# Moving the closing work of an attention unit to other steps of the next one

## The chip, the core and the metric

The kernel runs on one core of a Trainium2 chip. Its time is device time in microseconds (us), from the first to the last work of the program. The kernel before was run three times, 3617.6 to 3618.77 us, with a median of 3618.65 us. A profiled execution, which the profile describes, is one run more. The engines are TensorE (PE in the profile; PEld is its weight load), VectorE (DVE), ScalarE (ACT), GpSimd (POOL) and SyncE (SP, which here only starts DMAs).

## What is computed

Two graph layers over x of 8 batches, 2048 nodes and 256 features, all in float32. The first is a graph convolution with batch norm; the second is masked attention with 4 heads of 64. Each ends in a residual and a layer norm. Cut to what matters here:

```python
def _L1_gnn_ref(h, W, adj):
    qkv = h @ W                                   # 256 -> 3 x 256
    q, k, v = ...                                 # 4 heads of 64
    mask = jnp.where(adj == 0, -jnp.inf, 0.0)
    scores = einsum('bhid,bhjd->bhij', q, k) / np.sqrt(64) + mask
    attn = softmax(scores, axis=-1)
    return einsum('bhij,bhjd->bhid', attn, v)

x = _layernorm(x + _L0_gnn_ref(x, adj, ...))      # convolution, batch norm, twice
x = _layernorm(x + _L1_gnn_ref(x, L1_gnn_W, adj))
```

## The kernel before, in words

The convolution's part fills the first 1270 us or so and is not touched. The attention's part is cut into 64 units: 8 batches, in each of them 2 pairs of heads (`hp`), and for each pair 4 chunks (`c`) of 512 query rows. So a batch has eight units, which this text numbers 0 to 7: units 0 to 3 are the first pair's chunks, 4 to 7 the second pair's.

A unit has 16 steps, one for each tile of 128 keys. In a step TensorE makes the scores of the step three ahead (L842, into one of two `st` tiles in PSUM) and weighs the values with the exponentials of the present step (L872, into the single `out_ps` tile). Both use the array as four tiles of 64x64. VectorE adds the mask (L854), ScalarE takes the exponential (L860), in one of 13 `prob` tiles. The softmax uses no maximum; the sums of the exponentials are made on the side: an accumulating DMA started by GpSimd adds neighbouring steps' tiles in pairs (L882), GpSimd adds the pairs (L884, L891, L893) into `acc`, and TensorE adds over the partitions.

All four computing engines keep the order in which the program writes their work. A step is written as: scores, at step 15 the weighing and the result's copies (L897, L898), the masking, the exponentials, then the side tasks of that step, then the weighing, then the adding up. Side tasks are put in a table by `at_step(u, j, f, ...)`: task `f` belongs to step `int(j)` of unit `u`, and tasks of one step are ordered by `j`. A side task on TensorE therefore stands between the scores and the weighing of its step, and everything behind it on TensorE waits with it. The side tasks:

- Closing a unit, in the next one: `finish_sums` (L909, four products into the 32-column quarters, then ScalarE's copy into `sm`, L917), `finish_turn_sums` (two transposes L923, VectorE's copy L925 and reciprocal L930), `finish_turn` (four transposes L936 of the result) and `finish` (VectorE adds the scaled result to x1, L944, in halves).
- Closing a chunk of rows, after its second pair of heads: `emit_stats` (L660, L662 on VectorE, in halves), `root` (four small instructions on GpSimd, L97, L99, L667, L668) and `emit` (two applies L672 on ScalarE for each half, after the second one the output's DMA).
- Bringing in the next batch, a chunk at a time in units 3 to 7: `load_y` and `load_x` (DMAs on SP), `bn` (L696 on ScalarE, two), `norm` (four transposes L711 for each half, then VectorE's add L719 and the statistics), `root`, `apply` (L672) and `turn` (four transposes L740 for each half, then ScalarE's copy into `x1t`, L746).
- `project` (L777 for Q and K, L791 for V), at 0.1, 6.1 and 10.1 of a unit by the list `PROJECT`.

Every side product of TensorE goes into a PSUM tile named `pm`, of which there are two in turn: a third one has to wait until the first has been read. There are seven x1 tiles (`NCH + 3`), one `yt` tile and two `sm` tiles. In the last unit four of the 16 exponentials' tiles are summed by TensorE directly.

Of the kernel before, what the change touches and what calls it, by code (L numbers as in the profile page):

```python
# [8 lines left out]
F32 = mybir.dt.float32  # L9
# [17 lines left out]
def tile_gcn_then_masked_attention(  # L27
# [18 lines left out]
    P = 128  # L46
    B, N, D = x.shape
# [3 lines left out]
    NT = N // P  # L51
# [4 lines left out]
    NCH = N // CH  # L56
    TPC = CH // P
# [139 lines left out]
    with tc.tile_pool(name="bt7", bufs=1, side="right") as bp7, tc.tile_pool(  # L197
        name="stage", bufs=2, side="right"
    ) as sp, tc.tile_pool(name="stage1", bufs=1, side="right") as sp1, tc.tile_pool(
        name="pst", bufs=4, space=PSUM  # L200
# [80 lines left out]
    with tc.tile_pool(  # L281
        name="psa", bufs=4, space=PSUM
    ) as psa, tc.tile_pool(name="psh", bufs=3, space=PSUM) as psh, tc.tile_pool(
        name="psd", bufs=1, space=PSUM
# [94 lines left out]
        for v, (k, b, d) in enumerate(units):  # L379
            first, last = v == 0, v == len(units) - 1  # L380
            turn = not last and units[v + 1][0] != k
            w = v + 1
# [257 lines left out]
    BR = 256  # L640
# [168 lines left out]
    def attention():  # L809


        with tc.tile_pool(
            name="attn_in", bufs=2, side="left", reuse_waits="tile"
        ) as ip, ExitStack() as late, tc.tile_pool(
            name="ps_s", bufs=2, space=PSUM, reuse_waits="tile"
        ) as ps_s, tc.tile_pool(
            name="ps_o", bufs=1, space=PSUM, reuse_waits="tile"
        ) as ps_o, tc.tile_pool(
            name="ps_m", bufs=2, space=PSUM, reuse_waits="tile"
        ) as ps_m:  # L820
            inp = Layer1Input(ip, ps_m, NCH + 3)
            units = [(b, hp, c) for b in range(B) for hp in range(HP) for c in range(NCH)]
            probs, accs, outs, ots, sts, pms = {}, {}, {}, {}, {}, {}

# [5 lines left out]
            def on_pe(u):  # L830
                return 4 if u == NU - 1 else 0
# [68 lines left out]
            def finish_sums(u):  # L900

                pm = ps_m.tile([P, BR], F32, name="pm")
                parts = [probs.pop(g) for g in range((u + 1) * NT - on_pe(u), (u + 1) * NT)]
                parts.append(accs.pop(u))
                for n, part in enumerate(parts):
                    for h in range(2):
                        for q in range(2):
                            r0 = 32 * (2 * h + q)
                            nc.tensor.matmul(  # L909
                                pm[r0 : r0 + 32, :], ones[:, :32],  # L910
                                part[:, h, q * BR : (q + 1) * BR],
                                start=(n == 0), stop=(n == len(parts) - 1),
                            )
                for g in range(u * NT, (u + 1) * NT - on_pe(u)):
                    del probs[g]
                sts[u] = ap_.tile([P, BR], F32, name="sm")
                nc.scalar.copy(sts[u], pm)  # L917

            def finish_turn_sums(u):
# [50 lines left out]
            def at_step(u, j, f, *args):  # L970
                tasks = side.setdefault((u, int(j)), [])
                tasks.append((j, f, args))
                tasks.sort(key=lambda task: task[0])

            per_b = HP * NCH
            for u in range(NU):
                b, hp, c = units[u]
                at_step(u + 1, 4.1, finish_sums, u)
                at_step(u + 1, 6, finish_turn_sums, u)
                at_step(u + 1, 6.2, finish_turn, u)  # L980
                at_step(u + 1, 6.2, finish, u, 0)
                at_step(u + 1, 7, finish, u, 1)
                if u == NU - 2:
                    for half in range(2):
                        at_step(u + 1, 8.3 + half, inp.emit_stats, b, c, half)
                        at_step(u + 1, 13 + half, inp.emit, b, c, half)
                    at_step(u + 1, 10.5, inp.root, b, c)
                elif u == NU - 1:
                    for half in range(2):
                        at_step(u + 1, 6.3 + half, inp.emit_stats, b, c, half)  # L990
                        at_step(u + 1, 6.4 + half, inp.root_half, b, c, half)
                        at_step(u + 1, 8 + half, inp.emit_half, b, c, half)
                    at_step(u + 1, 10, count_sums)
                elif hp == HP - 1:
                    for half in range(2):
                        at_step(u + 1, 10.3 + 3 * half, inp.emit_stats, b, c, half)
                        at_step(u + 2, 3 + half, inp.emit, b, c, half)
                    at_step(u + 2, 2, inp.root, b, c)

            PROJECT = (0.1, 6.1, 10.1)

            def project_at(u, b, hp, c):
                for w in range(3):

                    later = 0
                    if w == hp == 0:
                        later = 10.1 if c == NCH - 1 else NT
                    at_step(u + (later == NT), PROJECT[w] + later % NT, inp.project, b, hp, c, w)  # L1010

            for b in range(B):
                u0 = b * per_b
                if b:
                    project_at(u0, b, 0, NCH - 1)
                for c in range(NCH):
                    project_at(u0 + 1 + c, b, 1, c)
                    if b + 1 == B:
                        continue
                    u = u0 + 3 + c  # L1020
                    at_step(u, 1, inp.load_y, b + 1, c)
                    at_step(u, 5, inp.load_x, b + 1, c)
                    for o in range(NO):
                        at_step(u, 5 + o, inp.bn, b + 1, c, o)
                    at_step(u, 10, inp.norm, b + 1, c, 0)
                    at_step(u + 1, 0, inp.norm, b + 1, c, 1)
                    at_step(u + 1, 4, inp.root, b + 1, c)
                    for half in range(2):
                        at_step(u + 1, 7 + half, inp.apply, b + 1, c, half)
                    at_step(u + 1, 10.2, inp.turn, b + 1, c, 0)  # L1030
                    at_step(u + 2, 4, inp.turn, b + 1, c, 1)
                    if c < NCH - 1:
                        project_at(u + 2, b + 1, 0, c)

# [13 lines left out]
            with tc.manual_schedule(engines=IN_ORDER):  # L1048
                for c in range(NCH):
                    inp.yt[0, c] = y0[c]  # L1050
                    inp.x1[0, c] = ip.tile([P, TPC, D], F32, name="x1", bufs=NCH + 3)
                    for o in range(NO):
                        inp.bn(0, c, o)

                def ready(c):
                    pm = ps_s.tile([P, TPC, D], F32, name="st")
                    for half in range(2):
                        pmh = pm[:, half * IT : (half + 1) * IT, :]
                        inp.turn_y(0, c, half, pmh)
                        inp.add_y(0, c, half, pmh, x0[c])  # L1060
                    inp.root(0, c)

                def halves(f, c):
                    for half in range(2):
                        f(0, c, half)

                for c in range(NCH - 1):
                    ready(c)
                halves(inp.apply, 0)
                halves(inp.turn, 0)  # L1070
                halves(inp.apply, 1)
                inp.project(0, 0, 0, 1, k_on_act=True)
                inp.project(0, 0, 0, 0)
                ready(NCH - 1)
                right.close()
                ap_ = inp.y_pool = late.enter_context(
                    tc.tile_pool(name="attn", bufs=2, side="right", reuse_waits="tile")
                )
                inp.project(0, 0, 0, 2)
                halves(inp.turn, 1)  # L1080
                for g in range(LEAD):
                    mask_scores(g, scores(g))
                    exps(g)
                    if g == 1:
                        inp.project(0, 0, 1, 1)
                        halves(inp.apply, 2)
                for g in range(NU * NT):
                    u, j = divmod(g, NT)
                    ahead = g + LEAD < NU * NT
                    if ahead:  # L1090
                        st = scores(g + LEAD)
                    if j == NT - 1:
                        weigh(g)
                        finish_out(u)
                    if ahead:
                        mask_scores(g + LEAD, st)
                        exps(g + LEAD)
                    for _, f, args in side.get((u, j), ()):
                        f(*args)
                    if j < NT - 1:  # L1100
                        weigh(g)
                    add_up(g)
                for u in (NU, NU + 1):
                    for j in range(NT):
                        for _, f, args in side.get((u, j), ()):
                            f(*args)
# [125 lines left out]
```

## Time and profile before

| | us |
|---|---|
| median of three runs | 3618.65 |
| the profiled execution | 3617.16 |
| its span, on which the profile's shares are taken | 3615.4 |
| TensorE matmuls busy | 3553.4 |
| GpSimd busy | 2267.2 |
| VectorE busy | 1985.4 |
| ScalarE busy | 1638.9 |
| a unit of the attention, depending on its side work | 35.1 to 38.1 |
| a unit of the last batch's second half, without projections | 29.7 to 32.0 |

The page of a profile gives each engine's busy time, the chain of work that ended last and the costliest groups of instructions. The list of waits says which group waited for which, with the sum, the number and the longest. The timeline lists instructions in order of time: start, duration, engine, line, operation, what it writes and reads, and in brackets the idle time before it and what ended it. The ends of matmuls are modelled and overlap the next ones, so times on TensorE are best read from start to start.

### The profile page before, as it was taken

To read this page: it belongs to the slowest core of one execution; us is meant where nothing else is said; L and a number is where in the kernel's file an instruction comes from. 1 tells how busy PE (TensorE), PEld (TensorE's weight loads), DVE (VectorE), ACT (ScalarE), POOL (GpSimd) and SP (SyncE) were. 2 spreads that over 40 slices of the span, in tenths; PEclk is the share of its full clock that TensorE was granted. 3 is DMA by queue.
4 is the path that set the end of the run, shared out by engine and by line. 5 is a ranking of instruction groups with operands and counts; after the bars stand their busy time and mean duration, and the time that the engine had idled before them with its cause. 6 is when DMAs were issued, how large, how long until landed. Compare 5 with 4: busy or idle time off the path is not lost.

```text
span 3615.4 us, 55155 instructions
## 1 busy us (share of the span) xinstructions
PE 3553.4 (98%) x22503; PEld 1468.3 (41%) x22503; DVE 1985.4 (55%) x2929; ACT 1638.9 (45%) x2036; POOL 2267.2 (63%) x1530
## 2 busy tenths in 40 slices
PE   8999999999999899999999999999999999999997
PEld 5444444444444443433333433343333333343332
DVE  6212141221146656766766776676676676676666
ACT  5101100110134455655665665565565565566555
POOL 3543263424247647776767686777777777777777
PEclk9999999999999999999999999999999999999999
DMA  9222232231246345656565566565656566555555
GB/s 337 70 70 87 81 134 82 76 99 29 82 190 263 143 91 107 125 123 123 114 143 112 117 134 129 112 139 119 117 123 133 113 127 131 117 118 123 111 109 115
DMA packets 197142, 440.14 MB, mean 122 GB/s; under 512 B 14080, under 2 KB 121104, under 8 KB 186384
## 3 DMA queue, kind: packets, MB, share of 16 engines
q0 software_dynamic: 64656, 239.37, 34.9%
q1 hardware_dynamic: 132048, 196.11, 15.8%
q8 instruction: 178, 2.92, 0.3%
q10 hardware_dynamic: 176, 1.06, 0.1%
q14 instruction: 84, 0.69, 0.1%
HBM read 126.62 MB, written 75.51 MB: 56 GB/s over the span
## 4 chain that ended last, share of the span: by engine, by line
PE 92%; ACT 3%; POOL 2%; DVE 2%; issue 1%; DMA 0%; POOLq 0%; ACTq 0%; SPq 0%; DVEq 0%
PE out_ps L872 23%; PE st L842 22%; PE pa L333 21%; PE pm L777 6%; PE ph L366 5%; PE pa L543 5%; PE pm L791 3%; PE pm L909 1%; PE pm L740 1%; ACT x L672 1%; DVE prob L854 1%; POOL acc L893 1%; ACT prob L860 1%; PE pm L711 1%; PE pm L936 1%; PE pm L923 1%
## 5 line engine op out<-in xcount | busy, mean ns | idle before, releaser
L854 DVE SCALAR_TENSOR_TENSOR prob<-mask,st 128x1024 f32<-128x1024 uint8 x1024 | 1241.1, 1218 | 588.0 <-PE st L842 585.0
L860 ACT ACTIVATE prob<-prob 128x1024 f32<-128x1024 f32 x1024 | 1079.5, 1056 | 910.9 <-DVE prob L854 795.5
L872 PE MATMUL out_ps<-prob,v 64*64 64x512 f32 x8192 | 1075.7, 595 | 1.7 <-DVE ot L898 1.7
L842 PE MATMUL st<-qt,kt 64*64 64x512 f32 x8192 | 1063.5, 589 | 1.7 <-DVE prob L854 1.3
L893 POOL TENSOR_TENSOR acc<-acc,prob 128x1024 f32<-128x1024 f32 x319 | 831.5, 2607 | 5.1
L333 PE MATMUL pa<-t,x 128*128 128x512 f32 x1792 | 772.1, 593 | 2.7 <-ACT x L309 2.7
L882 POOL DMA_DIRECT2D prob<-prob x447 | 403.1, 908 | 590.0 <-PE out_ps L872 518.8
L842 PEld LDWEIGHTS st<-qt,kt 64*64 64x64 f32 x8192 | 311.1, 133 | 572.9 <-issue 515.8
L333 PEld LDWEIGHTS pa<-t,x 128*128 128x128 f32 x1792 | 341.0, 190 | 431.8 <-issue 427.7
L872 PEld LDWEIGHTS out_ps<-prob,v 64*64 64x64 f32 x8192 | 287.5, 132 | 523.2 <-issue 453.8
L414 POOL TENSOR_TENSOR ag<-ag,dbc 128x512 f32<-128x512 f32 x16 | 20.2, 1262 | 484.9 <-DVE ag L413 452.2
L884 POOL TENSOR_TENSOR acc<-acc,prob 128x1024 f32<-128x1024 f32 x126 | 297.8, 2363 | 9.9
L370 ACT ACTIVATE h<-ph,b1s 128x512 f32<-128x512 f32 x112 | 76.9, 687 | 404.4 <-PE ph L366 404.4
L777 PE MATMUL pm<-x1t,wq 128*128 128x512 f32 x512 | 244.7, 601 | 0.7 <-ACT x1t L746 0.7
L394 ACT COPY ag<-pa 128x512 f32<-128x512 f32 x16 | 9.4, 585 | 421.5 <-PE pa L333 408.1
L366 PE MATMUL ph<-ag,w1s 128*128 128x512 f32 x448 | 193.4, 592 | 0.0
L891 POOL TENSOR_TENSOR acc<-prob 128x1024 f32<-128x1024 f32 x64 | 172.3, 2692 | 0.0
L672 ACT ACTIVATE x<-x,ln_nm,ln_rs 128x256 f32<-128x256 f32 x256 | 137.9, 587 | 31.9 <-POOL ln_nm L668 31.9
L371 DVE BATCH_NORM_STATS2 st<-h 128x6 f32<-128x512 f32 x112 | 76.9, 692 | 99.1 <-ACT h L370 99.1
L791 PEld LDWEIGHTS pm<-wq,x1t 128*128 128x128 f32 x1024 | 119.2, 192 | 28.5 <-issue 26.8
L366 PEld LDWEIGHTS ph<-ag,w1s 128*128 128x128 f32 x448 | 85.1, 190 | 107.1 <-issue 106.9
L791 PE MATMUL pm<-wq,x1t 128*128 128x128 f32 x1024 | 128.4, 278 | 0.0
(139 smaller groups left out, 2571.8 us busy)
## 6 DMA issues: line engine op xcount, KB each, us to landing
prob<-prob POOLq DMA_DIRECT2D x447, 512.0 KB, 4.7
x<-in_x_dram SPq DMA_DIRECT2D x92, 512.0 KB, 5.2
h_d<-h SPq DMA_DIRECT2D x28, 1024.0 KB, 3.9
t<-h_d SPq DMA_DIRECT2D x28, 1024.0 KB, 8.1
a<-in_adj_dram SPq DMA_DIRECT2D x16, 1024.0 KB, 5.0
y_d<-ag SPq DMA_DIRECT2D x32, 512.0 KB, 2.6
out_dram<-x SPq DMA_DIRECT2D x31, 512.0 KB, 5.9
yt<-y_d SPq DMA_DIRECT2D x28, 512.0 KB, 3.3
```

The costliest lines, as they stand in the source:

```text
L333: nc.tensor.matmul(pa, s.t[:, m, :], t[:, m, :], start=(m == 0), stop=(m == HT - 1))
L366: nc.tensor.matmul(ph, w1s[:, d, f * P : (f + 1) * P], ag[:, d, :], start=(d == 0), stop=(d == ND - 1),)
L543: nc.tensor.matmul(py, w[:, f, :], t[:, f, :], start=(f == 0), stop=(f == 1))
L777: nc.tensor.matmul(pm, wq[:, d, wcols], xt[:, d, cols], start=(d == 0), stop=(d == ND - 1))
L791: nc.tensor.matmul(pm[:, j * P : (j + 1) * P], xt[:, d, t * P : (t + 1) * P], wq[:, d, wcols], start=(d == 0), stop=(d == ND - 1),)
L842: nc.tensor.matmul(st[r * HD : (r + 1) * HD, h, :], kt[hs, j * P + r * HD : j * P + (r + 1) * HD], qt[hs, cols], start=True, stop=True,)
L854: nc.vector.scalar_tensor_tensor(p, mask[:, j, cols][:, None, :].to_broadcast([P, 2, CH]), MASKED, st, op0=ALU.mult, op1=ALU.add,)
L860: nc.scalar.activation(probs[g], probs[g], AF.Exp)
L872: nc.tensor.matmul(outs[u][hs, r, :], inp.qkv[b, hp][2][rs, j, hs], probs[g][rs, h, :], start=(j == 0), stop=(j == NT - 1),)
L882: nc.gpsimd.dma_start(probs[g - 1], probs[g], accum_op=ALU.add)
L884: nc.gpsimd.tensor_add(accs[u], accs[u], probs[g])
L893: nc.gpsimd.tensor_add(accs[v], accs[v], probs[g - 5])
```

## The change

It moves side tasks to other steps and changes two buffer counts. No instruction is added or taken away in the attention's work. In the next unit, the sums go from step 4 to step 6, their transposes and the result's from step 6 to step 10, around the V projection, and the additions to x1 from steps 6 and 7 to 10 and 11. A finished chunk's statistics go to steps 12 and 14, its root to step 15 of that same unit (before: step 2 of the next), its applies from steps 3 and 4 to 4 and 5. For the next batch's chunks, x is loaded at step 1 and not 5, `bn` goes to steps 3 and 4, the first half of `norm` from step 10 to 6, the root from 4 to 3, and both halves of `turn` to step 13 (before: step 10 and step 4 of the next unit). The Q projection of the first pair of heads is no longer put off. There are eight x1 tiles and one `sm` tile.

```diff
-            inp = Layer1Input(ip, ps_m, NCH + 3)
+            inp = Layer1Input(ip, ps_m, NCH + 4)
...
-                sts[u] = ap_.tile([P, BR], F32, name="sm")
+                sts[u] = ap_.tile([P, BR], F32, name="sm", bufs=1)
...
-                at_step(u + 1, 4.1, finish_sums, u)
-                at_step(u + 1, 6, finish_turn_sums, u)
-                at_step(u + 1, 6.2, finish_turn, u)
-                at_step(u + 1, 6.2, finish, u, 0)
-                at_step(u + 1, 7, finish, u, 1)
+                at_step(u + 1, 6, finish_sums, u)
+                at_step(u + 1, 10, finish_turn_sums, u)
+                at_step(u + 1, 10.2, finish_turn, u)
+                at_step(u + 1, 10.3, finish, u, 0)
+                at_step(u + 1, 11, finish, u, 1)
                 if u == NU - 2:
                     for half in range(2):
-                        at_step(u + 1, 8.3 + half, inp.emit_stats, b, c, half)
-                        at_step(u + 1, 13 + half, inp.emit, b, c, half)
-                    at_step(u + 1, 10.5, inp.root, b, c)
+                        at_step(u + 1, 11.3 + half, inp.emit_stats, b, c, half)
+                        at_step(u + 1, 14 + half, inp.emit, b, c, half)
+                    at_step(u + 1, 12.5, inp.root, b, c)
                 elif u == NU - 1:
                     for half in range(2):
-                        at_step(u + 1, 6.3 + half, inp.emit_stats, b, c, half)
-                        at_step(u + 1, 6.4 + half, inp.root_half, b, c, half)
-                        at_step(u + 1, 8 + half, inp.emit_half, b, c, half)
-                    at_step(u + 1, 10, count_sums)
+                        at_step(u + 1, 10.4 + half, inp.emit_stats, b, c, half)
+                        at_step(u + 1, 10.5 + half, inp.root_half, b, c, half)
+                        at_step(u + 1, 12 + half, inp.emit_half, b, c, half)
+                    at_step(u + 1, 14, count_sums)
                 elif hp == HP - 1:
                     for half in range(2):
-                        at_step(u + 1, 10.3 + 3 * half, inp.emit_stats, b, c, half)
-                        at_step(u + 2, 3 + half, inp.emit, b, c, half)
-                    at_step(u + 2, 2, inp.root, b, c)
+                        at_step(u + 1, 12.5 + 1.5 * half, inp.emit_stats, b, c, half)
+                        at_step(u + 2, 4 + half, inp.emit, b, c, half)
+                    at_step(u + 1, 15.5, inp.root, b, c)
...
             def project_at(u, b, hp, c):
                 for w in range(3):
-                    later = 0
-                    if w == hp == 0:
-                        later = 10.1 if c == NCH - 1 else NT
-                    at_step(u + (later == NT), PROJECT[w] + later % NT, inp.project, b, hp, c, w)
+                    at_step(u, PROJECT[w], inp.project, b, hp, c, w)
...
                     at_step(u, 1, inp.load_y, b + 1, c)
-                    at_step(u, 5, inp.load_x, b + 1, c)
+                    at_step(u, 1, inp.load_x, b + 1, c)
                     for o in range(NO):
-                        at_step(u, 5 + o, inp.bn, b + 1, c, o)
-                    at_step(u, 10, inp.norm, b + 1, c, 0)
+                        at_step(u, 3.5 + 1.2 * o, inp.bn, b + 1, c, o)
+                    at_step(u, 6.2, inp.norm, b + 1, c, 0)
                     at_step(u + 1, 0, inp.norm, b + 1, c, 1)
-                    at_step(u + 1, 4, inp.root, b + 1, c)
+                    at_step(u + 1, 3, inp.root, b + 1, c)
                     for half in range(2):
                         at_step(u + 1, 7 + half, inp.apply, b + 1, c, half)
-                    at_step(u + 1, 10.2, inp.turn, b + 1, c, 0)
-                    at_step(u + 2, 4, inp.turn, b + 1, c, 1)
+                        at_step(u + 1, 13 + 0.2 * half, inp.turn, b + 1, c, half)
```

More of the change, by code (lines that the diff above doesn't have):

```diff
@@ L1050, in attention @@
                     inp.yt[0, c] = y0[c]
-                    inp.x1[0, c] = ip.tile([P, TPC, D], F32, name="x1", bufs=NCH + 3)
+                    inp.x1[0, c] = ip.tile([P, TPC, D], F32, name="x1", bufs=NCH + 4)
                     for o in range(NO):
```

## The prediction

> **What bounds the kernel now.** I read the page's busy times and chain first, then the list of waits, then the timeline of single units of the attention, which start at 1272.8 us and fill the last 2343 us.
>
> ```profile
> PE 3553.4 (98%) x22503; PEld 1468.3 (41%) x22503; DVE 1985.4 (55%) x2929; ACT 1638.9 (45%) x2036; POOL 2267.2 (63%) x1530
> ...
> PE 92%; ACT 3%; POOL 2%; DVE 2%; issue 1%; DMA 0%; POOLq 0%; ACTq 0%; SPq 0%; DVEq 0%
> ```
>
> TensorE is the bound: only 62 us of the span are without a matmul, so a gain has to come from TensorE's few gaps and from what it loses between kinds of product. The waits name a gap that the change aims at, and one behind it:
>
> ```profile
> ACT x L672 <- POOL ln_nm L668: 31.9, 33, 4.8
> ...
> PE pm L923 <- ACT sm L917: 17.1, 31, 1.6
> ```
>
> The transposes of the sums (L923) wait for ScalarE's copy of the sums (L917). The timeline of one unit with input work gives the prices (start, duration; PE rows overlap, so I read start to start):
>
> ```profile
> 2020.31 1.04 PE L842 MATMUL st<-qt,kt 64*64 64x512 f32 x8
> ...
> 2021.16 1.04 PE L872 MATMUL out_ps<-prob,v 64*64 64x512 f32 x8
> ...
> 2022.02 1.04 PE L842 MATMUL st<-qt,kt 64*64 64x512 f32 x8
> ...
> 2022.99 0.64 PE L909 MATMUL pm<-acc,ones 128*32 128x256 f32 x8
> ...
> 2023.20 1.22 DVE L854 SCALAR_TENSOR_TENSOR prob<-mask,st 128x1024 f32<-128x1024 uint8 x1 [0.56 <-PE st L842]
> ...
> 2023.56 1.09 PE L872 MATMUL out_ps<-prob,v 64*64 64x512 f32 x8
> ...
> 2024.45 1.06 ACT L860 ACTIVATE prob<-prob 128x1024 f32<-128x1024 f32 x1 [0.68 <-DVE prob L854]
> 2024.47 1.04 PE L842 MATMUL st<-qt,kt 64*64 64x512 f32 x8
> ...
> 2025.42 0.35 ACT L917 COPY sm<-pm 128x256 f32<-128x256 f32 x1
> ...
> 2027.15 0.44 PE L923 MATMUL pm<-ident,sm 128*128 128x128 f32 x2
> ...
> 2027.43 1.88 PE L777 MATMUL pm<-x1t,wq 128*128 128x512 f32 x4
> ...
> 2029.15 0.60 PE L936 MATMUL pm<-ident,ot 128*128 128x128 f32 x4
> ...
> 2029.68 1.09 PE L872 MATMUL out_ps<-prob,v 64*64 64x512 f32 x8
> ```
>
> A plain step is 1.717 us (20.31 to 22.02). Any side product in it makes the scores 0.97 instead of 0.86 and the weighing 0.91 instead of 0.86: 0.16 us for leaving and re-entering the 64x64 shape. The sums take 0.57. From scores' start to the end of the sums' copy is 3.75 us (22.02 to 25.77), because ScalarE must first run that step's exponentials.
>
> [...] A projection alone takes 1.91, last in a group 1.81, in its middle 1.72; four transposes 0.44, plus 0.06 if first and 0.09 if last. [...]
>
> **The change, part by part**, in the execution profiled (3617.16 us; span 3615.4; the median of the runs, 3618.65, is 1.5 above it). I number the eight units of a batch 0 to 7; inputs of the next batch enter in units 3 to 7. Before, the first scores of batch 4's units start at 2450.77, 2488.82, 2524.66, 2559.76, 2595.25, 2631.57, 2667.50, 2704.67, and the next batch at 2741.44: 38.05, 35.84, 35.10, 35.49, 36.32, 35.93, 37.17, 36.77, together 290.67. Sixteen plain steps are 27.48; the rest is side work.
>
> Groups of side work. Before: steps 0, 4, 6, 10 in all eight units (32 per batch). After: 0, 6, 10 in all, 13 in units 4 to 7 (28). From these prices:
> - Step 0: Q projection 0.16 + 1.91 = 2.07 in units 0 to 3; with the transposes of norm's second half, 0.16 + 0.49 + 1.81 = 2.47 in units 4 to 7. Unit 5 gets the Q projection that now doesn't wait a unit (its own step 0 was bare and lost 0.84 to the result's copies, which a projection covers); unit 0 loses its second one.
> - Step 6: sums 0.57, then K projection. No row shows a projection right after the 128x32 sums: its entry costs 0 to 0.10. In the adjacency stage 16 transposes after such products take 1.90 (17.01 to 18.90) for 16 x 0.109 = 1.75, so entry and exit are paid there; I take 0.10. Units 0, 1, 2, 7: 0.16 + 0.57 + 1.91 = 2.64.
> - Step 10: sums' transposes 0.27, V projection 1.79, result's transposes 0.53, in and out 0.16: 2.75. The V projection lies between the sums' transposes and the result's, so the wait for VectorE's copy of the former is covered (it ends at 2.6 us of the step, needed at 3.0). Without it: 1.3 per unit, from 1.24 to 2.6.
> - Step 13: eight transposes, 0.16 + 1.02 = 1.18, units 4 to 7. ScalarE's two copies of them (0.58 each) end at 4.7 us, before step 14's exponentials can start at 5.3; if ScalarE were late there, the result's copy at step 15 would be late by as much.
>
> What goes: the wait at L923. The sums are copied at step 6 and needed at step 10, over 6 us later. In batch 4 that wait was 0.65, 0.74, 0.25 and 0.25 in units 0, 1, 6, 7.
>
> What is late next: in units 3 to 6 norm's first half is now at step 6, behind sums and K projection. It takes the third `pm` of that step, and there are two, so its transposes wait until the sums' tile is copied. They could start at 0.97 + 0.57 + 1.82 = 3.36 us; the copy ends at 3.75, they start at 3.80. Behind them stands the step's weighing, so TensorE stops. Step 6 adds 3.80 + 0.53 + 0.91 - 1.72 = 3.52 in units 3 to 5, where ScalarE is not behind (the two batch-norm activations, 0.80 each, are at steps 3 and 4, and a plain step leaves it about 0.7 us). In unit 6 the finished chunk's two applies (1.08 each) also fall at steps 4 and 5. From the exponentials of step 3, which start 2.72 before step 6: 0.97, 0.78, 0.97, 0.98, 0.78, 0.97, 0.98, 0.97, then the copy 0.35 ends at 5.04. Step 6 adds 5.09 + 0.53 + 0.91 - 1.72 = 4.81. Of this, 0.44 three times and 1.73 once are stall: 3.1 us per batch, as much as the old waits cost.
>
> After, then: units 0 to 2 are 27.48 + 2.07 + 2.64 + 2.75 = 34.94; unit 3 35.82; units 4 and 5 37.39; unit 6 38.68; unit 7 36.52. Sum 290.62 against 290.67: nothing. Batches 1 to 6 took 1747.2 before (three of them had a longer wait somewhere), 6 x 290.62 = 1743.7: -3.4. Batch 0, units 1 to 7: 256.0 before; after, with the Q projections at step 3 of units 1 and 2 that stay, 259.8: +3.8, since no finished chunk made it wait in units 0 and 1. Batch 7 has no inputs: units 0 to 4 179.2 before, 174.7 after: -4.5. Units 5 to 7 were 30.81, 32.00, 29.66; the sums' wait for the accumulator (0.57, as they stood at step 4) and the transposes' wait (1.18 in the last two) go: -0.5, -1.7, -1.75.
>
> The tail: the second-last chunk's root is moved from step 10 to 12 of the last unit, behind GpSimd's add of step 11 and ahead of its last two adds. It needs statistics which VectorE, with two maskings in between, ends at about 28 us of the unit; root 1.95, two adds 2.4 each: accumulator done at 35.0, before at 34.5 (3600.1). So unit 7 and tail end +0.5 and not -1.75.
>
> Costed at nothing: the root at step 15 puts 1.95 us ahead of GpSimd's last adds, done then 13.1 us after that step's start, and the sums ask at 14.1 or later; at the old step 4 it would have stalled them. It takes ScalarE's wait at L672 away. Loads of y and x both go out at step 1 on SP; the y lands in 3.1 to 5.6 us and is needed 9 us later. An eighth x1 buffer frees the x load from the output's DMA. One `sm` buffer: read four steps before it is rewritten. Statistics at steps 12 and 14 leave VectorE 1 us late at most, which the two `st` tiles just hold.
>
> Sum: -3.4 + 3.8 - 4.5 - 0.5 - 1.7 + 0.5 = -5.8, to 3611.4 for that execution and 3612.9 beside the median. With entry at 0, 3.2 lower.
>
> **Rivals.** (A) ScalarE is quicker than worked out, or norm's tile is free: no stall at step 6. Against it: exponentials precede the copy in ScalarE's order. It would save 21 x 0.44 + 7 x 1.73 = 21.4 more: 3591.5. (B) Slower: the same stall is deep in all four units as in unit 6, because a batch-norm activation waits for its y, now needed two steps earlier and loading beside x, and holds ScalarE's queue. That is 21 x 1.3 = 27 more: 3640. For it: 1 us of lateness there is 1 us of TensorE. It decides from a mean stall of 1.2 us (0.76 worked out), or a y landing over 9 us. Against: longest landing 5.6. (C) Fewer groups and waits do not show, as rows on TensorE were only redistributed: 3618.7.
>
> **Numbers.** Main case 0.66, A 0.10, B 0.20, C 0.04. A measurement tells about 0.2% (7.2 us) from nothing. The main case's own range is 3606 to 3620, with 0.38 of it beyond -7.2: faster 0.25 + 0.10 = 0.35, same 0.40 + 0.04 = 0.44, slower 0.21. The range for 8 in 10 is 3599 to 3632: it leaves out most of A and the upper half of B.
>
> **What would show it.** L923 waiting for L917 gone; the transposes of norm (L711) waiting for L917 28 times, about 21 us in all, longest 1.7; unit sums of 290.6; 28 fewer groups. It is wrong if L711 doesn't wait, if ScalarE waits for y, or if the accumulator is late at step 6.

## The result: the forecast effect, less than one measurement could tell from nothing

The changed kernel took 3614.6 us (median of four runs, 3613.77 to 3615.44), the kernel before 3618.56 (median of four). The ratio is 0.999, with a 95% interval of 0.9972 to 1.0007. The profiled execution took 3614.43 us, with a span of 3612.6. Its page (busy time, then the chain by engine, then the group of the applies):

```profile
PE 3553.4 (98%) x22503; PEld 1469.7 (41%) x22503; DVE 1994.5 (55%) x2929; ACT 1635.0 (45%) x2036; POOL 2265.8 (63%) x1530
...
PE 95%; ACT 2%; DVE 2%; POOL 1%; DMA 0%; issue 0%; DVEq 0%; POOLq 0%; ACTq 0%; SPq 0%
...
L672 ACT ACTIVATE x<-x,ln_nm,ln_rs 128x256 f32<-128x256 f32 x256 | 137.6, 586 | 10.5 <-POOL ln_nm L668 10.5
```

TensorE's busy time is that of before to the last digit, so the busy row tells nothing here. ScalarE's wait for the root, 31.9 us before, is 10.5. The list of waits (waiter <- releaser: us in all, times, longest) has the two that matter:

```profile
PEld pm L711 <- ACT sm L917: 38.9, 28, 2.2
...
PE pm L711 <- ACT sm L917: 15.7, 28, 1.4
...
PEld pm L923 <- ACT sm L917: 1.2, 1, 1.2
```

The transposes of the sums (L923) wait for the sums' copy once, in the tail, instead of 31 times. The transposes of `norm` (L711) wait for that same copy 28 times: the four units with inputs of seven batches. The weight load's 38.9 us count from its own last load, when products are still being made, and the matmul row's 15.7 depends on modelled ends (unit 6 of batch 4 has 2.23 and 1.40 in these rows, and 1.57 from start to start). What the wait costs is read from start to start below: 20 us.

First scores to first scores, the units 0 to 7 of each of the batches 1 to 6 take 34.94, 34.94, 34.94, 35.87, 37.45, 37.45, 38.57 and 36.52 us (within 0.01 in every batch), together 290.68; before, batch 4 had 290.67. So an undisturbed batch gains nothing, as forecast. Nearly all of what batches 1 to 6 gain comes from batches 2, 3 and 6, which took 291.70, 291.94 and 291.37 us before (291.77, 291.98 and 291.45 in experiment 1). The old wait was deeper there: in unit 0 of batch 2 and unit 7 of batch 3 GpSimd's additions, and with them its root, ended 1.1 and 1.3 us later than in the same units of batch 4, so that ScalarE's applies and the copy of the sums came later too, and L923 waited 1.59 and 1.46 us instead of 0.57 and 0.19. Why GpSimd was late in these batches stays open. The whole span, before against after:

| stretch | before | after | difference | forecast |
|---|---|---|---|---|
| up to the first scores of the attention | 1272.77 | 1275.34 | +2.57 | 0 |
| batch 0 | 303.68 | 307.56 | +3.88 | +3.8 |
| batches 1 to 6 | 1747.14 | 1744.05 | -3.09 | -3.4 |
| batch 7, units 0 to 4 | 179.19 | 174.69 | -4.50 | -4.5 |
| batch 7, units 5 and 6 | 62.81 | 60.47 | -2.34 | -2.2 |
| last unit and tail | 49.8 | 50.5 | +0.7 | +0.5 |

The head, which the change doesn't touch, took back two fifths of what the attention gained. In the timelines of before and then of after it is this line (start, duration), the projections of Q and K for the first unit, and the first scores behind it:

```profile
1264.14 3.70 PE L777 MATMUL pm<-x1t,wq 128*128 128x512 f32 x8 [0.67 <-ACT x1t L746]
...
1272.77 1.95 PE L842 MATMUL st<-qt,kt 64*64 64x512 f32 x16
```

```profile
1264.39 6.02 PE L777 MATMUL pm<-x1t,wq 128*128 128x512 f32 x8 [0.67 <-ACT x1t L746]
...
1275.34 1.95 PE L842 MATMUL st<-qt,kt 64*64 64x512 f32 x16
```

The same eight products take 2.3 us more; the mean granted clock from 1262 to 1280 us was 0.94 before and 0.80 after.

The step the forecast turned on is step 6. The timeline of after, batch 4: first unit 5 (the step begins at 2645.84), then unit 6 (it begins at 2683.28), in rows of TensorE and ScalarE:

```profile
2645.84 1.04 PE L842 MATMUL st<-qt,kt 64*64 64x512 f32 x8
...
2646.80 0.64 PE L909 MATMUL pm<-acc,ones 128*32 128x256 f32 x8
...
2648.27 1.06 ACT L860 ACTIVATE prob<-prob 128x1024 f32<-128x1024 f32 x1 [0.68 <-DVE prob L854]
2649.23 0.35 ACT L917 COPY sm<-pm 128x256 f32<-128x256 f32 x1
...
2649.64 0.66 PE L711 MATMUL pm<-ident,yt 128*128 128x128 f32 x4 [0.28 <-ACT sm L917]
2650.22 1.09 PE L872 MATMUL out_ps<-prob,v 64*64 64x512 f32 x8
...
2682.28 1.06 ACT L860 ACTIVATE prob<-prob 128x1024 f32<-128x1024 f32 x1
...
2683.24 1.08 ACT L672 ACTIVATE x<-x,ln_nm,ln_rs 128x256 f32<-128x256 f32 x2
2683.28 1.04 PE L842 MATMUL st<-qt,kt 64*64 64x512 f32 x8
2684.23 0.80 ACT L696 ACTIVATE yt<-yt,sh,sc 128x512 f32<-128x512 f32 x1
2684.25 0.64 PE L909 MATMUL pm<-acc,ones 128*32 128x256 f32 x8
...
2684.93 1.04 ACT L860 ACTIVATE prob<-prob 128x1024 f32<-128x1024 f32 x1
2685.88 1.07 ACT L672 ACTIVATE x<-x,ln_nm,ln_rs 128x256 f32<-128x256 f32 x2
...
2686.86 1.04 ACT L860 ACTIVATE prob<-prob 128x1024 f32<-128x1024 f32 x1
2687.81 0.34 ACT L917 COPY sm<-pm 128x256 f32<-128x256 f32 x1
2688.21 0.66 PE L711 MATMUL pm<-ident,yt 128*128 128x128 f32 x4 [1.40 <-ACT sm L917]
```

In unit 5 the transposes start 3.80 us into the step, as forecast; in unit 6, 4.93 (forecast 5.09). They could have started at 3.36, so the stalls are 0.44 three times and 1.57 once per batch, 2.9 us, and 20.3 in seven batches. In unit 6 the reason can be read off ScalarE's rows: the sums' products stop at 2684.8, and the copy that frees their tile starts 3 us later, behind an exponential, an apply of a finished chunk and one exponential more.

### The profile page after: what moved, and what is told of

It is laid out like the page before. It is cut to its first block, busy times and chain, and to the rows that moved or that the text cites. A ratio compares the mean times of both kernels' runs of the same rounds, so it can differ in the third digit from the quotient of the medians.

```text
span 3612.6 us, 55141 instructions
## 1 busy us (share of the span) xinstructions
PE 3553.4 (98%) x22503; PEld 1469.7 (41%) x22503; DVE 1994.5 (55%) x2929; ACT 1635.0 (45%) x2036; POOL 2265.8 (63%) x1530
## 3 DMA queue, kind: packets, MB, share of 16 engines
q10 hardware_dynamic: 176, 1.06, 0.1%
## 4 chain that ended last, share of the span: by engine, by line
PE 95%; ACT 2%; DVE 2%; POOL 1%; DMA 0%; issue 0%; DVEq 0%; POOLq 0%; ACTq 0%; SPq 0%
PE out_ps L872 25%; PE st L842 24%; PE pa L333 21%; PE ph L366 5%; PE pm L777 5%; PE pa L543 5%; PE pm L791 3%; DVE prob L854 1%; PE pm L711 1%; ACT prob L860 1%; PE pm L740 1%; PE pm L936 1%; PE pm L923 1%; PE ps L233 1%; PE pm L909 1%; PE ph L588 1%
## 5 line engine op out<-in xcount | busy, mean ns | idle before, releaser
L777 PE MATMUL pm<-x1t,wq 128*128 128x512 f32 x512 | 253.1, 617 | 0.7 <-ACT x1t L746 0.7
L944 DVE SCALAR_TENSOR_TENSOR x<-pm,ri,x 128x64 f32<-128x64 f32 x512 | 109.6, 277 | 62.4 <-PE pm L936 61.7
L672 ACT ACTIVATE x<-x,ln_nm,ln_rs 128x256 f32<-128x256 f32 x256 | 137.6, 586 | 10.5 <-POOL ln_nm L668 10.5
L777 PEld LDWEIGHTS pm<-x1t,wq 128*128 128x128 f32 x512 | 87.8, 191 | 119.8 <-issue 113.0
```

Source lines behind the costliest of these rows:

```text
L777: nc.tensor.matmul(pm, wq[:, d, wcols], xt[:, d, cols], start=(d == 0), stop=(d == ND - 1))
```

## The experiments

Three points were open: whether the head's 2.57 us are the change's; whether `norm` waits for the third tile (the theory) or is too early at step 6 for another reason (its y, the batch norm); and which of the other moves pays. A later place of the sums, of `norm` or of the applies tells these apart. Edits are against the changed kernel. "Attention" below is the time from the first scores of the first unit to those of the last one: 2292.83 before, 2286.77 after.

**1. The kernel before, profiled once more**

> The kernel before, profiled once more, for the start of the attention: in the kernel after, the first scores began at 1275.34 us and not at 1272.77, because the first two projections took 6.02 us for eight products and not 3.70, with the same instructions ahead. Theory 'clock': this is the TensorE clock granted at that place in an execution, so this run may show either value, 3.7 or 6.0. Theory 'change': it comes from the eighth x1 tile or the earlier loads, so this run shows 3.7 and a start within 0.5 us of 1272.8.

3620.12 us; the first scores start at 1274.64, the attention takes 2293.08, last unit and tail 50.6. The projections that took 3.70 us take 5.49 here. So the head differs by 1.9 us between two executions of one and the same kernel, and the tail by 0.8 (49.8 and 50.6). The changed kernel's order of the head shows both values as well: with the same eight x1 tiles and early loads the projections take 3.70 us in the profiled runs of experiments 2, 4, 7 and 8. Neither the +2.57 nor the +0.7 of the table can be put down to the change. What it does is in the attention's 63 units, -6.06 us.

**2. The two side tasks of step 6 in the other order**

```diff
-                at_step(u + 1, 6, finish_sums, u)
+                at_step(u + 1, 6.2, finish_sums, u)
...
-                    at_step(u, 6.2, inp.norm, b + 1, c, 0)
+                    at_step(u, 6, inp.norm, b + 1, c, 0)
```

> At step 6, norm's first half is put ahead of the K projection and the sums behind it. Theory 'tile' (norm's transposes wait for the copy of the sums, as the third of two pm tiles): no wait for that copy is left; step 6 of units 3 to 5 falls from 5.30 to about 4.75 us, and of unit 6 from 6.42 to about 5.6, where the second batch-norm activation becomes the last to be waited for (0.8 us). Per batch -2.5 us, seven batches -17: about 3597. Theory 'y' (the wait is really for the batch-normed y, ScalarE L696): the transposes stand earlier and wait longer, step 6 stays at 5.3 and 6.4 or grows, and the time is 3614 or more.

3593.78 us, ratio to before 0.9933 (0.992 to 0.9947); attention 2268.74. Nothing is removed; only the order within one step is turned, so that the sums take the third `pm` tile of the step, and the one they take over is that of `norm`, which VectorE reads (L719), not ScalarE behind its exponentials. Units 3 to 5 lose 0.54 each and unit 6 0.94. In unit 6 (which starts its step 6 at 2668.07) the timeline shows what is late next:

```profile
2668.03 1.08 ACT L672 ACTIVATE x<-x,ln_nm,ln_rs 128x256 f32<-128x256 f32 x2
...
2669.01 0.80 ACT L696 ACTIVATE yt<-yt,sh,sc 128x512 f32<-128x512 f32 x1
...
2669.87 0.55 PE L711 MATMUL pm<-ident,yt 128*128 128x128 f32 x3 [0.50 <-ACT yt L696]
2670.25 1.88 PE L777 MATMUL pm<-x1t,wq 128*128 128x512 f32 x4
...
2672.06 0.64 PE L909 MATMUL pm<-acc,ones 128*32 128x256 f32 x8
2672.63 1.09 PE L872 MATMUL out_ps<-prob,v 64*64 64x512 f32 x8
```

The transposes now wait for the batch norm (L696), which stands behind a finished chunk's applies (L672): 0.72 us, in unit 6 alone. The sums' products end the group, and the weighing follows them without a wait for their copy. The theory holds: the stall was the tile's.

**3. The sums back at step 4, by themselves**

```diff
-                at_step(u + 1, 6, finish_sums, u)
+                at_step(u + 1, 4.1, finish_sums, u)
```

> The sums alone go back to step 4, the rest stays as in the kernel after. Theory 'tile': norm at step 6 doesn't wait, so step 6 of units 3 to 6 is about 4.2 us; each unit has one more group of side work (+0.16 in units 0, 1, 2, 7). But the root at step 15 now stands ahead of GpSimd's last adds, so the sums of units 0, 1, 6, 7 should wait about 1.1 us for the accumulator at step 4. Per batch +2.6 us, in all about +16: 3630. If the root at step 15 costs nothing even there, those waits are missing, and the run ends at about 3600.

3625.98 us, a single run. Step 6 has two tiles again and falls to 4.23 us in units 3 to 6, as expected. But step 4 becomes a group of its own, and the sums come before the accumulator is ready. The list of waits:

```profile
PEld pm L909 <- POOL acc L893: 63.5, 48, 4.1
...
PE pm L909 <- POOL acc L893: 23.5, 20, 3.6
```

After has the second row once (3.6, in the tail). I expected these waits in units 0, 1, 6 and 7, about 1.1 us each; regularly they are in units 0 and 1 (0.3 and 1.5). The likely reason, which no run tests: after units 4 to 7 the transposes at step 13 have given GpSimd 1.2 us more, which covers units 5 to 7 and all but 0.3 of 1.5 us in unit 0. Batch 0 is 2.0 us faster and batches 1 to 6 are 2.9 slower together, where 2.6 each was expected; the last batch, without inputs and hence with no stall to lose, is 10 slower, 4.3 of it in the last unit and the tail. So step 6 for the sums is right, and its gain lies mostly in the last batch.

**4. The first half of `norm` back at step 10**

```diff
-                    at_step(u, 6.2, inp.norm, b + 1, c, 0)
+                    at_step(u, 10, inp.norm, b + 1, c, 0)
```

> Norm's first half alone goes back to step 10, the rest stays as in the kernel after. Theory 'tile': the wait at step 6 is gone (2.64 us of side work in all units), but at step 10 the V projection becomes the third of two pm tiles and waits about 0.9 us for VectorE's copy of the turned sums: step 10 of units 3 to 6 about 5.8 us and not 4.47. Per batch +0.6 us, +4 in all: about 3618. Theory 'more groups or waits elsewhere': step 10 about 4.9 without a wait, and the run at about 3597.

3614.17 us, a single run; attention 2289.72, 2.95 more than after, in a run whose head was 2.7 shorter. Step 6 is 4.36 in all units, as in units 0, 1, 2 and 7 of the changed kernel: the stall is gone from there, and a plain step's 1.72 and the forecast's 2.64 make 4.36, so that the projection's entry behind the 128x32 products is confirmed at 0.10. But step 10 now has four tiles, and the list of waits shows the same rule with another reader:

```profile
PEld pm L791 <- DVE sums_all L925: 23.9, 28, 0.9
...
PE pm L791 <- DVE sums_all L925: 17.3, 28, 0.6
```

The V projection (L791), third there, waits for VectorE's copy of the sums' transposes. The stall follows the third tile, not the task.

**5. A finished chunk's applies at steps 1 and 2**

```diff
-                        at_step(u + 2, 4 + half, inp.emit, b, c, half)
+                        at_step(u + 2, 1 + half, inp.emit, b, c, half)
```

> The kernel after, with a finished chunk's applies and its output at steps 1 and 2 and not 4 and 5. Theory 'tile' says that unit 6 waits 1.1 us longer than units 3 to 5 at step 6 only because these two applies stand before the copy of the sums in ScalarE's order: step 6 of unit 6 falls from 6.42 to about 5.3, the unit from 38.57 to about 37.5; all others stay. Seven batches: -7.8 us, about 3606.5. If unit 6 is late for another reason (its y, its root), it stays at 38.6.

3606.37 us, ratio 0.997 (0.9959 to 0.998). Unit 6 falls from 38.57 to 37.51 and its step 6 from 6.42 to 5.36, nearly the 5.30 of the others; no other unit of batches 1 to 6 moves. The deep stall of unit 6 was ScalarE's queue: these applies, and nothing in `norm` itself.

**6. The root back at step 2 of the next unit**

```diff
-                    at_step(u + 1, 15.5, inp.root, b, c)
+                    at_step(u + 2, 2, inp.root, b, c)
```

> The kernel after, with a finished chunk's root back at step 2 of the next unit. The prediction costed the new place at nothing: with the applies at steps 4 and 5 the root would be done in time either way. Expected: every unit within 0.1 us of the kernel after, 3614.5. The rival is that the place of the root is what took away ScalarE's waits for it: then unit 6 and its step 6 grow by up to 2 us a batch, +14 at most.

3613.87 us, ratio 0.9984 (0.9977 to 0.9991); no unit differs from after by more than 0.01. The root's place, which the change names, is worth nothing. Since its units are those of after, these runs also measure the change once more, against 38 runs of the kernel before on that chip (3619.37): 5.5 us faster.

**7. The Q projection of the first pair put off as before**

```diff
-                    at_step(u, PROJECT[w], inp.project, b, hp, c, w)
+                    later = 0
+                    if w == hp == 0:
+                        later = 10.1 if c == NCH - 1 else NT
+                    at_step(u + (later == NT), PROJECT[w] + later % NT, inp.project, b, hp, c, w)
```

> The kernel after, with the Q projections of the first pair of heads put off as before. Unit 5's step 0 is bare again: it loses its projection (1.82) and about 0.86 returns as waits at steps 0 to 2, so unit 5 falls by about 1.0 us. Unit 0 has a second Q projection at step 10, which as the fourth pm tile there waits about 0.6 us for ScalarE's copy of V: +2.4. Per batch +1.4, in all about +10: 3624.

3623.64 us, ratio 1.0012 (1.0003 to 1.0021); batches 1 to 6 are 1.38 longer each. Unit 0 pays 2.35: the projection, 1.91, and 0.43 at step 10, where the last chunk's projection comes fourth and waits until ScalarE has copied the V projection's tile, the second (L777 waits for L798 seven times). Unit 5 gets back 0.97 only, since its step 0 without a projection waits for the result's copies.

**8. The turns at steps 10 and 4, as before, on top of 7**

```diff
-                        at_step(u + 1, 13 + 0.2 * half, inp.turn, b + 1, c, half)
+                    at_step(u + 1, 10.2, inp.turn, b + 1, c, 0)
+                    at_step(u + 2, 4, inp.turn, b + 1, c, 1)
```

> The kernel after, with the two halves of x1's transposes at step 10 and at step 4 of the next unit, and the first pair's Q projections put off, as before: a Q projection at step 0 needs both halves. From the prices: step 13 of units 4 to 7 loses 1.18; step 10 there gains about 1.1 (0.44 and a wait of about 0.65 for the copy of V, as the fourth pm tile); step 4 of units 5, 6, 7 and 0 gains 0.75 as a group of its own; the put-off projections +1.4 a batch as measured; the copies at step 4 make the wait for the sums' copy up to 0.6 longer. Per batch +4.0 to +5.0, in all +28 to +35: about 3646. If the two halves' places cost nothing, it is the +9 of the put-off projections alone: 3624.

3636.79 us, ratio 1.005 (1.0027 to 1.0073); against experiment 7 the batches 1 to 6 are 2.06 longer each. Step 10 takes 5.49 instead of 4.47, with a wait of 0.43 at its fourth tile, the turn's, for the copy of V (0.65 expected), and step 4 takes 0.74 for a group of its own. I expected 3646, 4.0 to 5.0 us a batch above the kernel after; it is 3.4. The waits at step 10 were shallower, and step 6 of unit 6, expected up to 0.6 longer, is 0.27 shorter (6.15 instead of 6.42). The turns were not put back alone, since the Q projection at step 0 needs both halves: what their places are worth is known only together with experiment 7's.

**9. Seven x1 tiles, and x loaded at step 5**

```diff
-            inp = Layer1Input(ip, ps_m, NCH + 4)
+            inp = Layer1Input(ip, ps_m, NCH + 3)
...
-                    at_step(u, 1, inp.load_x, b + 1, c)
+                    at_step(u, 5, inp.load_x, b + 1, c)
...
-                    inp.x1[0, c] = ip.tile([P, TPC, D], F32, name="x1", bufs=NCH + 4)
+                    inp.x1[0, c] = ip.tile([P, TPC, D], F32, name="x1", bufs=NCH + 3)
```

> The kernel after, with x loaded at step 5 again and seven x1 tiles. The prediction costed the earlier load and the eighth tile at nothing. That held for the old place of norm. With norm's first half at step 6, theory 'enabler': in unit 6 the x1 tile to be loaded is the one whose output goes out at step 5, so x lands some 12 us after step 5, VectorE's addition of norm waits for it with the masking queued behind, and TensorE stops: unit 6 grows by 5 to 9 us, the others stay within 0.5 us. Seven batches: +35 to +60, about 3660. If the load is hidden anyway, the run ends at 3614.5.

3681.81 us, ratio 1.0177 (1.0147 to 1.0206), more than expected. Only unit 6 changes, by 9.7 us: `norm` at step 6 adds to an x that is still loading (the list of waits, then four windows of batch 4's unit 6: after the length and the busy times of PE, PEld, DVE, ACT and POOL with their counts comes the granted clock, then the DMA share and the GB/s).

```profile
DVE x L719 <- DMA x<-in_x_dram: 69.7, 7, 10.4
```

```profile
2725.00:2732.00 7.00, 5.59 (x47) 1.91 (x45) 0.69 (x1) 2.25 (x5) 2.45 (x2) 1.00 0.97 216
2732.20:2739.30 7.10, 0.21 (x4) 0.00 (x0) 2.79 (x7) 0.00 (x0) 3.83 (x3) 0.88 0.88 185
2739.30:2743.20 3.90, 3.85 (x20) 1.29 (x24) 2.35 (x2) 3.87 (x6) 0.00 (x0) 0.50 0.01 2
2743.20:2747.00 3.80, 3.80 (x30) 2.42 (x22) 1.50 (x3) 2.01 (x4) 0.00 (x0) 0.84 0.00 0
```

The maskings stand behind that addition on VectorE, so TensorE stops for 7 us (second line). Then the granted clock is 0.50 (third line), and the next steps take 2.6 us more; that was not in the expectation. With `norm` at step 6, going without the buffer and the earlier load costs 67 us. Whether the two would bring anything with `norm` at its old step no run tests.

**10. The best of these together**

The edits of experiments 2 and 5, and at the end the second-last chunk's root behind GpSimd's last additions and its applies behind the last unit's sums. Only the new edit is shown:

```diff
-                        at_step(u + 1, 14 + half, inp.emit, b, c, half)
-                    at_step(u + 1, 12.5, inp.root, b, c)
+                        at_step(u + 2, 7 + half, inp.emit, b, c, half)
+                    at_step(u + 2, 5, inp.root, b, c)
```

> Norm's first half ahead of the sums at step 6, as in the run with both exchanged, and a finished chunk's applies at steps 1 and 2; the second-last chunk's root and applies behind the last unit's sums. Theory 'tile': no wait of norm is left, unit 6 is 36.9 us like units 4 and 5 (37.63 in the run with the exchange alone), seven batches -5.0; and the last accumulator is done 2 us earlier in the last unit, so the tail is about 2 us shorter. Together about 3587, some 7 us below the exchange alone.

3587.65 us, ratio 0.9913 (0.9899 to 0.9926): 0.9% faster than before, and faster than the changed kernel, whose units ran at 0.9984 in the same comparison (experiment 6). Attention 2264.42, unit 6 37.01. The tail, first of after (last unit's scores from 3562.11) and then of this version (from 3538.93):

```profile
3589.93 0.23 POOL L97 TENSOR_SCALAR ln_rs<-ln_mv 128x4 f32<-128x4 f32 x1 [0.39 <-DVE ln_mv L662]
...
3591.82 4.78 POOL L893 TENSOR_TENSOR acc<-acc,prob 128x1024 f32<-128x1024 f32 x2
...
3596.66 0.81 PE L909 MATMUL pm<-acc,ones 128*32 128x256 f32 x8 [3.60 <-POOL acc L893]
...
3598.47 1.06 PE L936 MATMUL pm<-ident,ot 128*128 128x128 f32 x4
```

```profile
3565.21 4.84 POOL L893 TENSOR_TENSOR acc<-acc,prob 128x1024 f32<-128x1024 f32 x2 [0.18 <-DMA prob<-prob]
...
3570.10 0.64 PE L909 MATMUL pm<-acc,ones 128*32 128x256 f32 x8 [0.23 <-POOL acc L893]
3570.13 0.23 POOL L97 TENSOR_SCALAR ln_rs<-ln_mv 128x4 f32<-128x4 f32 x1
```

GpSimd's last two additions no longer stand behind a root; TensorE's wait for them is 0.23 instead of 3.60, and the last unit with the tail takes 46.3 instead of 50.5, 4.2 us less where about 2 were expected. That the total still meets the expected 3587 is in part chance: in the profiled executions the head was 2.5 us longer here than in experiment 2.

## Why the prediction was right

Forecast were 3612.9 us and 5.8 less than before; measured are 3614.6 and 4.0 less. These four runs alone can't tell that from nothing (the interval reaches 1.0007). What bears the forecast out is the two profiled executions, which are 2.7 apart: the 63 units give 6.06, where the terms of the forecast for them add up to 6.3, while the head, forecast at 0, takes 2.57 back and the tail 0.7.

- *The price list.* A unit without inputs, 34.94 forecast, 34.94 measured, in every batch from the second on; unit 7 36.52 and 36.52. The entry of a projection behind the sums, 0 to 0.10 by its bounds, is 0.10 (experiment 4).
- *What is late next.* The wait moved from L923 to L711 with the number forecast (28) and nearly the size: 20.3 us against 21.4. The mechanism was put to the test by changing the order (2), by moving the reader (4) and by emptying ScalarE's queue (5), and each did what the theory of the third tile asks for. The longer waits of three batches, which the prediction counted as gone without saying what they were, were the old wait at L923 too, as the batches 2 and 3 above show.
- *Two small terms of it were off.* Behind their wait the four transposes took 0.586 instead of 0.53, which makes units 3 to 5 35.87 and 37.45 rather than 35.82 and 37.39. And in unit 6 I added up ScalarE's instructions with 0.17 us too much (the copy's tile is free 4.93 us into the step and not 5.09), 38.57 rather than 38.68. The two cancel: 290.68 against 290.62.
- *The tail.* The accumulator was to be done 0.5 us later than before, at 35.0 of the last unit; it was done at 34.5, as before. The +0.7 measured comes behind it, where products ran slower (L936 1.06 us at a granted clock of 0.50, before 0.60 us at 1.00). As experiment 1 shows 0.8 between two executions of one kernel, the agreement with the +0.5 is chance.
- *Costed at nothing.* Right for the root (6). For the eighth tile and the early load "nothing" holds while both are there, as the unit sums show; what they cover is 67 us (9). The load and the buffer were taken away together, and which of them would do alone stays open, as do the `sm` buffer and the places of the statistics, which weren't tried.
- *The rivals.* A, no stall, was refuted by the waits, but is what experiment 10 comes to: 3591.5 forecast for it, 3587.65 there with 4.2 from the tail. B didn't happen: `norm` never waited for y in the changed kernel. C fits the first interval, but not the time of the 63 units (-6.06) nor the interval of experiment 6. Where the change's gain went is step 6: of what it saved elsewhere, 20.3 us were spent there again, and experiment 2 gets 18.0 of them back in the 63 units.

## What to carry to other kernels

When several side tasks are gathered in one slot, count the tiles they take in turn and ask who reads each of them: the first task beyond the pool waits for a reader in *its* engine's order, and putting the tile with the slow reader last in the slot can be worth more than all the moving. An engine with slack on average can still be the one that is late in one slot, where several of its tasks fall together: ScalarE, 45% busy here, made step 6 stall 1.57 us in unit 6 and 0.44 in the units 3 to 5. And a tile or a load that "costs nothing" should be taken away once, since it may be what holds the rest up.

## What the runs showed of the hardware

The same eight projections at the end of the convolution's part took 3.70 us in five of the twelve profiled executions and 5.49 to 6.12 in the other seven, with the kernel before among both (3.70, and 5.49 in experiment 1), and so moved the time by up to 2.4 us. The mean granted clock over them was 1.00 in the profiled execution of before (1264.14 to 1267.84 us) and 0.61 in that of after (1264.39 to 1270.41). Both traces have a stretch at 0.50 here: from 1250.4 to 1264.0 us before, so that it ends just ahead of the projections, and from 1248.6 to 1269.1 after, over most of them. In both it begins while TensorE waits 5.9 us (L711 for L696), a wait that ends at 1251.30 before and at 1251.54 after. What sets the beginning and the length of such a stretch is not shown; no run varied it.

A granted clock of 0.50 bears on two more readings. In experiment 9 it follows TensorE's stop of 7 us, with scores and weighing at 3.46 us a step instead of 1.72. In the tail of after, L936 took 1.06 us at 0.50, behind TensorE's wait of 3.60 us for the accumulator; in the first execution of before it took 0.60 at 1.00, behind a wait of 2.96. But the second execution of before (experiment 1) has 1.06 us behind the same 2.96, and experiment 4 has 0.88 behind 3.60. So the length of the wait alone didn't tell how long the products behind it took.

For the reader it means that a gain below 3 us of this kernel (the head moved by up to 2.4, the tail by 0.8) is to be looked for in unit sums, which repeat within 0.01 us in the changed kernel's batches, and not in totals.
